# Layer 1 of a two-layer graph network: three gather tiles, two one-hot and message tiles, and new distances between its stages

## The chip, the core and the metric

The kernel runs on one core of a Trainium2 chip. A core has five engines, each with its own instruction queue worked through in order: TensorE (PE in the profile, with its weight loads as PEld), VectorE (DVE), ScalarE (ACT), GpSimd (POOL) and SyncE (SP, which here issues transfers only). Transfers are issued from the queues of SP, ACT and POOL. Engines wait for each other through semaphores. The metric is the device time of one execution in microseconds.

## The reference

There are 12,500 nodes with 48 features and 200,000 edges, sorted by their target node `dst`. Two layers follow each other, each ending in a residual sum and a layer norm over the features:

```
h   = relu(concat(x[dst], x[src], edge_attr_32) @ W1 + b1)
x   = layernorm(x + segment_sum(h @ W2 + b2, dst))            # layer 0
m   = relu(x[src] + edge_attr_48)
x   = layernorm(x + (1 + eps) * x + segment_sum(m, dst))      # layer 1
```

The change is in layer 1: for every edge a row of x (after layer 0) is gathered by `src`, the edge's 48 features are added, relu is taken, and the results are summed by `dst`.

## The kernel before

Edges are worked in 391 groups of 512: 128 partitions by 4 tiles (`TPC`). Nodes are worked in 14 segments of 896 (`SN`). Each layer is one call of `run(stages, ...)` (L485 on): a loop over iterations k, in which every stage (f, d) is called with group g = k - d, in the order of the list. The list thus writes out the order of the instructions of every engine by hand; the tile pools add the waits. A pool with n buffers of a name hands them out in turn, and whoever writes a buffer waits until the readers of its last use, n uses ago, are done.

Layer 0 gathers x rows (L222, by `fetch0`), multiplies and sums, and `finish0` (L395) ends a segment: the new rows x1 are stored to `x1_dram` by SP, and for all but the last segment also to `front_dram` by ACT.

Layer 1 has these stages:

- `fetch1(g)`: four indirect gathers on POOL (all have line L222), one for each tile of the group, into a tile `xs`. Groups 0 to 5 (`FRONT`) are gathered from `front_dram`, which lacks the last segment, so that they need not wait for it; these 24 gathers are issued near the end of layer 0. All others read `x1_dram`. `xs` has 12 buffers.
- `fill1(g)`: a one-hot matrix `hot` of the group's targets, on DVE (L530), ten buffers; and the group's edge features, which SP loads in chunks of five groups (`load_edges`, L314, tile `e48c`, three buffers). DVE reads `rel1` and `iota_1`, both in SBUF.
- `message1(g)`: m = xs + e48c on DVE (L539), for groups 0 to 5 a second add of `more` (L541), then the relu on ACT into `msg1` (L543), ten buffers.
- `sum1(g)`: four matmuls of `msg1` and `hot` on PE (L557; the profile counts two passes of each, eight rows) into a PSUM bank that twelve groups share (`GB`); a bank is opened and closed by a matmul of zeros (L554, L562).
- `drain1(g)`: for the last group of a bank, its columns are added or copied into `table` by DVE (L575) and ACT (L580). When a segment is complete, `finish1` follows: transposes on PE (L362), sums and layer norm on DVE with two steps on ACT (L420 to L390), and the store by SP (L425).

`lead1` is called at the end of an iteration. At k = -1, 1 and 3 it calls `last_segment` for two groups each: for the six front groups it looks up the rows of the last segment, which `front_dram` lacks, by one-hots `which_e` on DVE (L600), transposes on PE (L605), comparisons `o` on DVE (L621), matmuls (L613, L623) and a reduction `more` on DVE (L629). Eight iterations before a segment's last group it loads that segment's x1 rows (`load_seg`, L163).

The stages before stand in the order fetch1 (6 groups ahead), fill1 (2 ahead), sum1 (1 behind), drain1 (9 behind), message1 (0).

Of the kernel before, what the change touches and what calls it, by code (L numbers as in the profile page):

```python
# [27 lines left out]
F32 = mybir.dt.float32  # L28
# [6 lines left out]
P = 128  # L35
# [3 lines left out]
D = 48  # L39
# [6 lines left out]
TPC = 4  # L46
# [10 lines left out]
TAIL = 128  # L57
SROWS = HEAD + SN + TAIL
AHEAD = 6
NW = 8  # L60
EC = 5
R1 = 48
GB = 12
FRONT = 6
# [9 lines left out]
W1 = STEP + 2 * R1  # L74
# [19 lines left out]
def seg_of(g):  # L94
    return min(share(g) // SN, NSEG - 1)
# [10 lines left out]
@with_exitstack  # L106
def gnn_kernel(
    ctx: ExitStack,
    tc: tile.TileContext,
    x: bass.AP,  # L110
    src: bass.AP,
    dst: bass.AP,
    e32: bass.AP,
    e48: bass.AP,
    w1: bass.AP,
    b1: bass.AP,
    w2: bass.AP,
    b2: bass.AP,
    eps: bass.AP,
    out: bass.AP,  # L120
):
    nc = tc.nc
    flag_pool = ctx.enter_context(tc.tile_pool(name="flag", bufs=1))
    dram = ctx.enter_context(tc.tile_pool(name="dram", bufs=1, space=bass.MemoryType.DRAM))
    flag = flag_pool.tile([1, 1], I32, name="flag")
    with ExitStack() as fast:
        windowed(fast, tc, dram, flag, x, src, dst, e32, e48, w1, b1, w2, b2, eps, out)
    misfit = nc.values_load(
        flag, engines=[mybir.EngineType.PE, mybir.EngineType.DVE, mybir.EngineType.Activation,
                       mybir.EngineType.Pool, mybir.EngineType.SP],  # L130
        min_val=0, max_val=4 * P,
    )
    with tc.If(misfit > 0), ExitStack() as slow:
        general(slow, tc, dram, x, src, dst, e32, e48, w1, b1, w2, b2, eps, out)


def windowed(ctx, tc, dram, flag, x, src, dst, e32, e48, w1, b1, w2, b2, eps, out):
    nc = tc.nc
    const = ctx.enter_context(tc.tile_pool(name="const", bufs=1))
    cats = ctx.enter_context(tc.tile_pool(name="cats", bufs=AHEAD + 8))  # L140
    echunk = ctx.enter_context(tc.tile_pool(name="echunk", bufs=3))
    xs_pool = ctx.enter_context(tc.tile_pool(name="xs_pool", bufs=AHEAD + FRONT))
    late = ctx.enter_context(tc.tile_pool(name="late", bufs=10))
    work = ctx.enter_context(tc.tile_pool(name="work", bufs=3))
    aggs = ctx.enter_context(tc.tile_pool(name="aggs", bufs=3))
    node = ctx.enter_context(tc.tile_pool(name="node", bufs=2))
# [22 lines left out]
    nc.scalar.dma_start(w1a, w1[0:D, :])  # L169
    wcats = [const.tile([Q, HID], F32, name=f"wcat{k}") for k in range(NW)]  # L170
    for t in wcats:
# [41 lines left out]
    x1_dram = dram.tile([NPAD, D], F32, name="x1_dram")  # L213
# [7 lines left out]
    def gather(t, table, g, j):  # L221
        nc.gpsimd.indirect_dma_start(  # L222
            out=t, out_offset=None, in_=table,
            in_offset=bass.IndirectOffsetOnAxis(
                ap=src_i[:, g * TPC + j : g * TPC + j + 1], axis=0
            ),
        )
# [81 lines left out]
    def load_edges(name, table, width, g):  # L309
        c = g // EC  # L310
        if g % EC == 0:
            n = min(EC, NCHUNK - g)
            chunk[name] = echunk.tile([P, EC, TPC * width], F32, name=name)
            nc.sync.dma_start(  # L314
                chunk[name][:, :n, :],
                table[g * CHUNK : (g + n) * CHUNK, :].rearrange(
                    "(c p t) d -> p c (t d)", p=P, t=TPC
                ),
            )
        return chunk[name][:, g % EC, :].rearrange("p (t d) -> p t d", t=TPC)  # L320
# [10 lines left out]
    def start_of(engine, g):  # L331
        if (engine, g // 4) not in starts_of:
            kind = {nc.sync: mybir.EngineType.SP, nc.vector: mybir.EngineType.DVE}[engine]
            _, starts_of[engine, g // 4] = nc.values_load_multi_w_load_instructions(
                off[0:1, g // 4 * 4 : g // 4 * 4 + 4], engines=[kind], min_val=0,
                max_val=SROWS - W,
                skip_runtime_bounds_check_because="off is held to its range where it is made",
            )
        return starts_of[engine, g // 4][g % 4]
# [52 lines left out]
    def rows_of(table, s):  # L392
        return table[s * SN : (s + 1) * SN, :].rearrange("(t p) d -> p t d", p=Q)
# [42 lines left out]
    cat, h, pt, ph, pm, pa, hot = {}, {}, {}, {}, {}, {}, {}  # L436

    def fetch0(g):
        cat[g] = cats.tile([P, TPC, Q], F32, name="cat")
        for j in range(TPC):  # L440
            gather(cat[g][:, j, W : W + D], x, g, j)

    def fill0(g):
# [3 lines left out]
        nc.sync.dma_start(  # L447
            wcats[g % NW][0:W, :], a_dram[seg_of(g)][bass.ds(start_of(nc.sync, g), W), :]
        )
# [10 lines left out]
    def hidden0(g):  # L460
        ph[g] = psum.tile([HID, TPC, P], F32, name="ph", bufs=2)
        nc.tensor.matmul(ph[g], wcats[g % NW], h[g], start=True, stop=True)  # L462

# [21 lines left out]
    def run(stages, adds, finish, lead):  # L485


        last = max(d for _, d in stages)
        first = min(d for _, d in stages)
        for k in range(first, NCHUNK + last):  # L490
            for f, d in stages:
                g = k - d
                if 0 <= g < NCHUNK:
                    f(g)
                    if f is adds:
                        for s in finishes.get(g, []):
                            finish(s)
            lead(k)

    def lead0(k):  # L500
        for s in range(1, NSEG):
            if k == first_group(s - 1) + 4:
                load_seg(x, s)
            if k == first_group(s - 1) + 8:
                project(s)
        if k == 14:
            check_windows()
            nc.scalar.dma_start(rows_of(front_dram, NSEG - 1), none)
        if k == NCHUNK - AHEAD:
            for g in range(FRONT):  # L510
                fetch1(g, front_dram)

    def fetch1(g, table):
        cat[g] = xs_pool.tile([P, TPC, D], F32, name="xs")
        for j in range(TPC):
            gather(cat[g][:, j, :], table, g, j)

    for g in range(AHEAD):
        fetch0(g)
    project(0)  # L520
    run(
        [(lambda g: g >= AHEAD and fetch0(g), -AHEAD), (fill0, -2), (add0, 7), (sum0, 6),
         (bias0, 5), (message0, 4), (relu0, 3), (hidden0, 2), (turned0, 1), (turn0, 0)],
        add0, finish0, lead0,
    )


    def fill1(g):
        o = late.tile([P, TPC, W1], F32, name="hot")
        nc.vector.tensor_tensor(  # L530
            o, iota_1[:, None, :].to_broadcast([P, TPC, W1]),
            rel1[:, g, :, None].to_broadcast([P, TPC, W1]), op=ALU.is_equal,
        )
        hot[g] = o
        h[g] = load_edges("e48c", e48, D, g)

    def message1(g):
        m = work.tile([P, TPC, D], F32, name="m")
        nc.vector.tensor_tensor(m, cat.pop(g), h[g], op=ALU.add)  # L539
        if g in more:  # L540
            nc.vector.tensor_tensor(m, m, more.pop(g), op=ALU.add)  # L541
        msg = late.tile([P, TPC, D], F32, name="msg1")
        nc.scalar.activation(msg, m, AF.Relu)  # L543
        h[g] = msg

# [92 lines left out]
    def lead1(k):  # L638
# [4 lines left out]
                load_seg(x1_dram, s)  # L643

    run(
        [(lambda g: g >= FRONT and fetch1(g, x1_dram), -AHEAD), (fill1, -2), (sum1, 1), (drain1, 9), (message1, 0)],
        None, None, lead1,
    )

# [210 lines left out]
```

## Time and profile before

| | before |
|---|---|
| median of 3 runs | 3965.46 us (3963.3 to 3965.85) |
| profiled execution | 3967.04 us, its span 3965.3 us |
| POOL busy in the span | 2989.5 us (75%), 3138 instructions |
| PE busy | 2559.0 us (65%) |
| DVE busy | 1093.3 us (28%) |
| ACT busy | 560.3 us (14%) |
| granted PE clock, whole span | 0.645 of full |

The span runs from the first to the last instruction of the program. Layer 0 takes its first half; the gathers of layer 1 run from 1967.2 us to 3947.4 us. A row of a group gives its line, engine, operation and tiles, then how often it ran, busy microseconds, the mean of one in nanoseconds, and after the second bar how long the engine stood idle just before these instructions and what ended it. A row of the timeline gives the start, the duration, the engine, the line and the tiles, and in brackets the idle time before it and what ended it. A row of the waits names the engine and line that waited, what it waited for, the sum in microseconds, how often, and the longest. "issue" is time in which an engine waited for nothing that the profile shows.

### The profile page before, as it was taken

To read this page: it belongs to the slowest core of one execution; us is meant where nothing else is said; L and a number is where in the kernel's file an instruction comes from. 1 tells how busy PE (TensorE), PEld (TensorE's weight loads), DVE (VectorE), ACT (ScalarE), POOL (GpSimd) and SP (SyncE) were. 2 spreads that over 40 slices of the span, in tenths; PEclk is the share of its full clock that TensorE was granted. 3 is DMA by queue.
4 is the path that set the end of the run, shared out by engine and by line. 5 is a ranking of instruction groups with operands and counts; after the bars stand their busy time and mean duration, and the time that the engine had idled before them with its cause. 6 is when DMAs were issued, how large, how long until landed. Compare 5 with 4: busy or idle time off the path is not lost. (4 is left out here: it accounts for less than half of the span.)

```text
span 3965.3 us, 40239 instructions
## 1 busy us (share of the span) xinstructions
PE 2559.0 (65%) x12586; PEld 1748.8 (44%) x12586; DVE 1093.3 (28%) x2766; ACT 560.3 (14%) x1329; POOL 2989.5 (75%) x3138
## 2 busy tenths in 40 slices
PE   6888888888888888888874444444444444444444
PEld 4565555555555555555553333232233233333232
DVE  4233233323323332332252221222122222222122
ACT  1122112212212221221110000000000000000000
POOL 7777777777777777777777777777777777777776
PEclk8777787777778777877765555555555555555555
DMA  3122222212212221221121211111111121122121
GB/s 77 36 54 48 48 42 48 50 37 52 50 42 49 48 49 37 52 47 36 35 58 35 48 43 35 43 43 43 40 43 43 30 53 43 30 48 44 34 48 28
DMA packets 309612, 175.26 MB, mean 44 GB/s; under 512 B 124288, under 2 KB 309136, under 8 KB 309392
## 3 DMA queue, kind: packets, MB, share of 16 engines
q0 software_dynamic: 100096, 77.07, 11.2%
q1 hardware_dynamic: 179632, 84.47, 7.8%
q10 hardware_dynamic: 29664, 11.10, 1.1%
q8 instruction: 100, 1.64, 0.2%
q14 instruction: 120, 0.98, 0.1%
HBM read 157.37 MB, written 15.03 MB: 43 GB/s over the span
## 5 line engine op out<-in xcount | busy, mean ns | idle before, releaser
L222 POOL DMA_INDIRECT cat<-in_x_dram,src_i x1564 | 1483.2, 948 | 480.6 <-issue 336.8
L222 POOL DMA_INDIRECT xs<-x_dram,src_i x1540 | 1481.0, 962 | 469.3 <-issue 360.2
L557 PE MATMUL pt<-hot,msg 128*48 128x128 f32 x3128 | 743.7, 419 | 1059.7 <-ACT msg L543 1059.5
L557 PEld LDWEIGHTS pt<-hot,msg 128*48 128x48 f32 x3128 | 561.9, 194 | 1273.5 <-ACT msg L543 1249.7
L462 PE MATMUL ph<-cat_t,wcat 128*128 128x512 f32 x782 | 573.3, 824 | 0.9 <-DVE cat_t L458 0.9
L454 PE MATMUL pt<-ident,cat 128*128 128x128 f32 x1564 | 399.4, 348 | 266.8 <-DMA cat<-in_x_dram,src_i 261.7
L454 PEld LDWEIGHTS pt<-ident,cat 128*128 128x128 f32 x1564 | 263.9, 174 | 668.8 <-DMA cat<-in_x_dram,src_i 411.2
L539 DVE TENSOR_TENSOR m<-xs,e48c 128x192 f32<-128x192 f32 x391 | 146.2, 374 | 1433.3 <-DMA xs<-x_dram,src_i 1433.3
L471 PE MATMUL pm<-w_sb,h 128*128 128x48 f32 x3128 | 531.4, 323 | 1.8 <-ACT h L466 1.8
L458 DVE COPY cat_t<-pt 128x512 f32<-128x512 f32 x391 | 269.8, 690 | 883.1 <-PE pt L454 883.1
L471 PEld LDWEIGHTS pm<-w_sb,h 128*128 128x128 f32 x3128 | 478.0, 234 | 27.8 <-ACT h L466 2.1
L466 ACT ACTIVATE h<-ph,b_sb 128x512 f32<-128x512 f32 x391 | 268.4, 686 | 1340.1 <-PE ph L462 1306.6
L543 ACT ACTIVATE msg<-m 128x192 f32<-128x192 f32 x391 | 141.9, 363 | 1714.9 <-DVE m L539 1661.8
L530 DVE TENSOR_TENSOR hot<-iota,rel 128x512 f32<-128x512 f32 x391 | 266.5, 682 | 0.0
L354 PE MATMUL pa<-cat,msg 128*48 128x48 f32 x3128 | 260.6, 237 | 2.1 <-DVE agg L349 2.0
L354 PEld LDWEIGHTS pa<-cat,msg 128*48 128x48 f32 x3128 | 207.4, 147 | 77.1 <-issue 46.8
L475 DVE TENSOR_TENSOR msg<-pm,b_sb 128x192 f32<-128x192 f32 x391 | 139.2, 356 | 275.0 <-PE pm L471 274.8
L462 PEld LDWEIGHTS ph<-cat_t,wcat 128*128 128x128 f32 x782 | 153.4, 244 | 1.2 <-DVE cat_t L458 1.2
L323 DVE TENSOR_TENSOR cat<-iota_w,rel 128x192 f32<-128x192 f32 x391 | 136.2, 350 | 0.1
L445 ACT ACTIVATE cat<-e32c 128x128 f32<-128x128 f32 x391 | 117.0, 300 | 43.6 <-DMA e32c<-in_e_dram 14.2
L349 DVE TENSOR_TENSOR agg<-agg,pa 48x48 f32 x391 | 74.3, 190 | 17.0 <-PE pa L354 10.3
L293 PE MATMUL px<-w1a,xt 48*128 48x128 f32 x196 | 47.2, 407 | 20.2 <-ACT xt L290 20.2
(90 smaller groups left out, 607.0 us busy)
## 6 DMA issues: line engine op xcount, KB each, us to landing
e48c<-in_e_dram SPq DMA_DIRECT2D x78, 480.0 KB
cat<-in_x_dram,src_i POOLq DMA_INDIRECT x1564
e32c<-in_e_dram SPq DMA_DIRECT2D x78, 320.0 KB
xs<-x_dram,src_i POOLq DMA_INDIRECT x1540
wcat<-a SPq DMA_DIRECT2D x391, 24.0 KB
a<-a ACTq DMA_DIRECT2D x14, 256.0 KB
a<-a ACTq DMA_DIRECT2D x14, 192.0 KB
x_seg<-in_x_dram SPq DMA_DIRECT2D x14, 168.0 KB
```

Of the source, the lines that this page charges most:

```text
L222: nc.gpsimd.indirect_dma_start(out=t, out_offset=None, in_=table, in_offset=bass.IndirectOffsetOnAxis(ap=src_i[:, g * TPC + j : g * TPC + ...
L354: nc.tensor.matmul(pa, msg[:, j, :], hot[:, j, :], start=j == 0, stop=j == TPC - 1)
L454: nc.tensor.transpose(pt[g][:, j, :], cat[g][:, j, :], ident[:P, :P])
L458: nc.vector.tensor_copy(h[g], pt.pop(g))
L462: nc.tensor.matmul(ph[g], wcats[g % NW], h[g], start=True, stop=True)
L466: nc.scalar.activation(h[g], ph.pop(g), AF.Relu, bias=b1_sb)
L471: nc.tensor.matmul(pm[g][:, j, :], h[g][:, j, :], w2_sb, start=True, stop=True)
L475: nc.vector.tensor_tensor(h[g], pm.pop(g), b2_sb[:, None, :].to_broadcast([P, TPC, D]), op=ALU.add)
L530: nc.vector.tensor_tensor(o, iota_1[:, None, :].to_broadcast([P, TPC, W1]), rel1[:, g, :, None].to_broadcast([P, TPC, W1]), op=ALU.is_equal,)
L539: nc.vector.tensor_tensor(m, cat.pop(g), h[g], op=ALU.add)
L543: nc.scalar.activation(msg, m, AF.Relu)
L557: nc.tensor.matmul(bank[k][:, i * STEP : i * STEP + W1], msg[:, j, :], o[:, j, :], start=False, stop=False, skip_group_check=True,)
```

## The change

It touches layer 1 alone. Groups 0 to 5 get six gather tiles of their own name (`xs_front`); the others share three tiles `xs`, and their gathers stand two groups ahead in the order. `hot` and `msg1` come from a pool with two buffers each instead of ten. The edge load is a stage of its own, five groups ahead. The one-hot stands one group ahead instead of two, the sum in the message's own iteration and behind it, the drain three groups behind instead of nine, and behind message and sum instead of ahead of the message.

```diff
+AHEAD1 = 2
...
-    xs_pool = ctx.enter_context(tc.tile_pool(name="xs_pool", bufs=AHEAD + FRONT))
-    late = ctx.enter_context(tc.tile_pool(name="late", bufs=10))
+    xs_pool = ctx.enter_context(tc.tile_pool(name="xs_pool", bufs=AHEAD1 + 1))
+    pair = ctx.enter_context(tc.tile_pool(name="pair", bufs=2))
...
     def fetch1(g, table):
-        cat[g] = xs_pool.tile([P, TPC, D], F32, name="xs")
+        if g < FRONT:
+            cat[g] = xs_pool.tile([P, TPC, D], F32, name="xs_front", bufs=FRONT)
+        else:
+            cat[g] = xs_pool.tile([P, TPC, D], F32, name="xs")
...
+    def load1(g):
+        h[g] = load_edges("e48c", e48, D, g)
+
     def fill1(g):
-        o = late.tile([P, TPC, W1], F32, name="hot")
+        o = pair.tile([P, TPC, W1], F32, name="hot")
...
         hot[g] = o
-        h[g] = load_edges("e48c", e48, D, g)
...
-        msg = late.tile([P, TPC, D], F32, name="msg1")
+        msg = pair.tile([P, TPC, D], F32, name="msg1")
...
     run(
-        [(lambda g: g >= FRONT and fetch1(g, x1_dram), -AHEAD), (fill1, -2), (sum1, 1), (drain1, 9), (message1, 0)],
+        [(load1, -5), (lambda g: g >= FRONT and fetch1(g, x1_dram), -AHEAD1), (fill1, -1),
+         (message1, 0), (sum1, 0), (drain1, 3)],
         None, None, lead1,
     )
```

## The prediction

> **What bounds the kernel now.** I read the page first, then the waits, then the timeline, at the hand-over between the layers and in layer 1. From the page:
>
> ```profile
> span 3965.3 us, 40239 instructions
> L222 POOL DMA_INDIRECT xs<-x_dram,src_i x1540 | 1481.0, 962 | 469.3 <-issue 360.2
> L530 DVE TENSOR_TENSOR hot<-iota,rel 128x512 f32<-128x512 f32 x391 | 266.5, 682 | 0.0
> L539 DVE TENSOR_TENSOR m<-xs,e48c 128x192 f32<-128x192 f32 x391 | 146.2, 374 | 1433.3 <-DMA xs<-x_dram,src_i 1433.3
> ```
>
> The gathers of layer 1 take 1481.0 us and the 0.3 us of issue before each another 469.3: 1950 us, nearly the whole of the layer. DVE sits 1433.3 us waiting for gathered rows. So POOL's queue is the bound, and a microsecond in which POOL cannot issue is lost, as nothing after it has slack. The list of waits asks whether POOL ever waits for a buffer:
>
> ```profile
> DVE m L539 <- DMA xs<-x_dram,src_i: 1433.3, 362, 6.0
> POOL xs L222 <- DVE m L539: 3.0, 10, 0.3
> ```
>
> It does not: ten entries of 0.3 us, which is its issue time. With twelve xs tiles, the gathers of group g need m of group g-12. Now the hand-over, in order of time:
>
> ```profile
> 2007.51 2.23 DVE L600 TENSOR_SCALAR which_e<-iota,part,block 128x128 bf16<-128x128 f32 x8
> 2008.65 1.43 PE L605 MATMUL pa<-ident,which_e 128*128 128x128 bf16 x8
> 2012.49 0.94 POOL L222 DMA_INDIRECT xs<-x_dram,src_i  x1 [0.30 <-issue]
> 2023.92 0.35 DVE L539 TENSOR_TENSOR m<-xs,e48c 128x192 f32<-128x192 f32 x1
> 2024.58 0.68 DVE L530 TENSOR_TENSOR hot<-iota,rel 128x512 f32<-128x512 f32 x1
> 2024.70 0.36 ACT L543 ACTIVATE msg<-m 128x192 f32<-128x192 f32 x1 [16.71 <-DVE m L541]
> 2025.12 1.94 PE L557 MATMUL pt<-hot,msg 128*48 128x128 f32 x8 [0.33 <-ACT msg L543]
> 2025.85 2.13 DVE L600 TENSOR_SCALAR which_e<-iota,part,block 128x128 bf16<-128x128 f32 x8
> 2040.43 1.07 PE L557 MATMUL pt<-hot,msg 128*48 128x128 f32 x8
> 2044.07 0.35 DVE L539 TENSOR_TENSOR m<-xs,e48c 128x192 f32<-128x192 f32 x1
> 2045.27 1.44 POOL L222 DMA_INDIRECT xs<-x_dram,src_i  x1 [0.30 <-issue]
> ```
>
> Gathers from x1_dram start at 1997.41, four to a group, 1.25 us apart; counting them, the row at 2012.49 is the first of group 9. Counting the m rows from 2005.59 (group 0), 2023.92 is m of group 2 and 2044.07 m of group 6. The rows with which_e open the three look-ups of the last segment, some 16 us each, which hold DVE and PE until 2041. Here POOL ran far ahead of m: group 9 was issued 31 us before m of group 6. Last, a steady group and the end of a segment:
>
> ```profile
> 2060.41 0.94 POOL L222 DMA_INDIRECT xs<-x_dram,src_i  x1 [0.30 <-issue]
> 2066.69 0.36 DVE L539 TENSOR_TENSOR m<-xs,e48c 128x192 f32<-128x192 f32 x1 [4.04 <-DMA xs<-x_dram,src_i]
> 2196.20 0.51 DVE L420 TENSOR_TENSOR total<-px,x_seg 128x336 f32<-128x336 f32 x1 [2.57 <-PE px L362]
> 2200.24 0.51 DVE L390 TENSOR_TENSOR o<-ln_yc,ln_rstd 128x336 f32<-128x336 f32 x1
> 2201.15 1.29 POOL L222 DMA_INDIRECT xs<-x_dram,src_i  x1 [0.30 <-DVE m L539]
> ```
>
> 2060.41 is the first gather of group 18 and 2066.69 its m: 6.28 us from one to the other. A group takes four gathers, 4 x 1.25 = 5.0 us.
>
> **The change, part by part.** Layer 0 and the 24 front gathers keep their order and their tiles; 0.
>
> *Three xs tiles, at the hand-over.* Groups 0 to 5 have tiles of their own, groups 6, 7 and 8 find three free ones, and group 9 must wait for m of group 6. That wait is new. Without anything else m(6) ends at 2044.07 + 0.35 = 2044.42. With 0.30 of issue POOL starts group 9 at 2044.72 and not at 2012.49: 32.2 us, a floor, since the three look-ups are not shortened.
>
> *Two hot tiles.* The one-hot of group g now waits until PE has summed group g-2, and it stands on DVE ahead of m(g-1). So behind m(2), DVE waits for ACT and PE before the next one-hot and m(3). From the rows: m(2) 2023.92, ACT 2024.70 (0.78 later, the second add between), PE 2025.12 (0.42), sum 1.94, and 0.05 to the next start (an estimate from PE-to-DVE gaps of 0.03 to 0.06 in the timeline): 3.19 us, where before the next one-hot started 0.66 after m. That is 2.53 us more, or 1.66 where the sum takes 1.07, as at 2040.43. Before m(6) it happens four times: between m(0) and m(1), m(2) and m(3), m(4) and m(5), m(5) and m(6). In the other places the sum lies ahead of a look-up and is long done. I take the first two at 1.94 and the last two at 1.07, as the rows at these times have them: 2 x 2.53 + 2 x 1.66 = 8.4.
>
> *Sum at distance 0.* PE now sums the second group of a pair ahead of the next look-up's transposes. Before, these began 1.14 us after which_e (2007.51 to 2008.65). Now the sum ends 0.78 + 0.42 + 1.94 = 3.14 after m and which_e starts 0.66 after m, so they begin 2.48 after it: 1.3 later, for the second and the third look-up: 2.6. Bounds 0 and 2.6.
>
> *One-hot at -1 instead of -2.* One one-hot fewer stands ahead of the first look-up: minus 0.6 (their pitch there).
>
> So m(6) ends at 2044.42 + 8.4 + 2.6 - 0.6 = 2054.8, POOL starts group 9 at 2055.1, and the new wait is **42.6 us**. With all four sums slow it is 44.3; with all fast and no late transposes 38.3.
>
> *After it.* m(7) follows m(6) by a one-hot that waits for a sum, some 3.5 us, and m(8) as much later; the gathers of groups 10 and 11, 5.0 us apart, find their tiles free. So one stall, not a series. What was late before is regained in part: from 2012.49 to 2055.23 the gathers of groups 9 to 16 took 42.7 us for 32 x 1.25 = 40.0, five of them 1.44 us long, because DVE ran one-hots and adds end to end. DVE is paced by PE now; I leave 0.7 for chance collisions: minus 2.0 (0 to minus 2.8).
>
> *Steady groups.* POOL needs m(g-3) when it starts group g: 3 x 5.0 = 15.0 us after group g-3 began, and m ends 6.28 + 0.36 = 6.6 after that. 8.4 us of margin. DVE's new loop is m to ACT 0.45, to PE 0.42, sum 1.94, 0.05, one-hot 0.6: 3.5 us in a group of 5.0, hidden; if that cover went, every group would pay the excess. For msg1's two tiles ACT waits for a sum that is two groups old: 0.
>
> *Where the one-hot falls.* A gather that starts while a two-input DVE instruction runs is held until about 0.13 us before its end: a one-hot at 2200.94, 0.68 long, held the gather of 2201.15 to 1.29 us instead of 0.94. Before, it ran 0.3 us behind m; now 2.85 us behind it (0.45 + 0.42 + 1.94 + 0.05). m starts close to the start of a gather, so 2.85 - 2 x 1.25 = 0.35 into a later one, and it is done at 1.03, before the next start at 1.25: no hold. Added up over the timeline of before, the gathers that a one-hot held lost 8 us in all of layer 1, mostly behind late m's; sums late by a bank change will collide now and then. I take minus 2, bounds minus 8 and plus 15 (374 groups by 0.04 us, if all sums took 1.07 and the one-hot ended at 1.98 + 0.68 = 2.66, where the next gather starts at 2.50).
> The Trainium skill, SBUF — State Buffer, section Who interferes with whom, says that a DVE instruction with two SBUF inputs contends with a GpSimd instruction that reads SBUF and that whoever comes first keeps the ports for its whole instruction. The trace agrees for a gather that comes second; but one-hots run inside a 0.94 us gather, and m is lengthened to 0.43 us at most. By the rule a one-hot 0.35 into a gather would start at its end, 0.94, and hold the next until 1.63, not 1.25: 0.38 x 374 = 142 us slower, and the sum would be 4146; by the rows it is nothing.
>
> *Segment ends.* Thirteen times a finish blocks DVE. It now follows m(k) and its sum: sum done at 2.81, transposes 1.0, then total to o (2196.20 to 2200.75) 4.6, so DVE is free 8.4 us after m(k) started; the one-hot 0.6, and m(k+1) starts at 9.0 instead of 5.0. 4.0 late against 8.4 of margin, and 1.5 made up per group: 0. If the cover went, 13 times the excess.
>
> *Edge loads five ahead, drains three behind.* SP issues 79 loads earlier in its order, ahead of x_seg loads and out stores that they stood behind; no m waits for e48c in the list of waits, the load still waits for m of eleven groups before, and 11 groups are 55 us: 0. A drain three groups behind its sum comes over 10 us after it: 0. The tail after the last gather keeps its chain: 0.
>
> Sum: 42.6 - 2.0 - 2 = +38.6. The profiled execution took 3967.04 (span 3965.3), 1.6 over the median of the runs, 3965.46. I put the difference on the median: **4004**. Its own range: stall 38.3 to 44.3, give or take 2 for PE's clock in the look-ups, regained 0 to 2.8, one-hots minus 8 to plus 15: 3991 to 4027.
>
> **Rivals.**
> - *The one-hot meets gather starts.* PE's clock or the phase of m shifts it. For: 2201.15 shows the hold; the sum takes 1.07 at times. Against: granted clock 0.51 over 2055 to 3945, where nearly all sums take 1.94. A one-hot that fell anywhere would be in the way 0.51/1.25 of the time by 0.26 us on average, 0.106 x 374 = 40 us: 4044.
> - *Segment ends stall POOL.* If m(k+1) is over 8.4 us late, 13 times the excess; twice the 4.0 that I count and another 2 for a slow landing (DVE's longest wait for rows is 6.0, the usual one 4.2) gives 1.6 x 13 = 21 us: 4025.
> - *Not slower.* The place is the POOL row of layer 1: 962 ns mean against 944 in an undisturbed gather, 18 ns x 1540 = 28 us. If pacing took all of it, the stall would have to be under 28 to break even; its floor is 32.2. It would be a wash only at 3965.5 + 32.2 - 28 = 3970 at best. That group 9 does not wait for m(6) at all, which would mean no change, has only the order of buffers against it, and that is plain.
>
> **How the numbers follow.** Main case 0.83, one-hot collisions 0.08, segment ends 0.05, not slower 0.04 (0.02 for each side). Faster 0.02, same (within 0.2%, 8 us, about what a measurement of this kernel can tell) 0.02, slower 0.96. The range is the main case's own, a microsecond wider at the top: 3991 to 4028 leaves out the first rival's 40 us.
>
> **What would show it.** POOL idle once, about 43 us from 2012.5, ended by DVE m; x_dram gathers back to back afterwards, with no further waits for m above 1 us; DVE's one-hots waiting for PE sums at L557's successor; the mean of a gather between 944 and 975 ns; the last gather about 39 us later than 3946.5. The forecast is wrong if POOL waits for m at segment ends, or if that mean passes 975.

## The result, and the profile after

The changed kernel takes 4005.68 us, median of four runs (4003.38 to 4010.75), against 3965.65 us before (3963.3 to 3966.2): a ratio of 1.0103, with a 95% interval of 1.009 to 1.0116. The forecast was 4004 us, with a range of 3991 to 4028. The profiled execution took 4003.38 us, the fastest of the four; its span is 4001.4 us. The profile before is of an execution of 3967.04 us, so the two profiles differ by 36.1 us in their spans where the medians differ by 40.0.

Lines in the profile after have moved: L223 is the gather (before L222), L537 the one-hot (L530), L545 m (L539), L549 the relu (L543), L563 the sum (L557), L606 which_e (L600), L611 its transposes (L605), L421 to L391 the end of a segment (L420 to L390).

From the page of the changed kernel:

```profile
span 4001.4 us, 40613 instructions
L223 POOL DMA_INDIRECT xs<-x_dram,src_i x1540 | 1480.2, 961 | 508.1 <-issue 299.3
L537 DVE TENSOR_TENSOR hot<-iota,rel 128x512 f32<-128x512 f32 x391 | 270.7, 692 | 942.7 <-PE pt L563 942.7
```

A gather is as long as before, 961 ns against 962. What POOL idled ahead of its gathers grew from 469.3 to 508.1 us. The one-hot, which never waited, now waits 942.7 us for PE, and DVE has that time: its wait for gathered rows falls from 1433.3 to 489.5 us. The list of waits of the changed kernel says where POOL's 39 us are, as engine, line, what it waited for, and then the sum, the number and the longest:

```profile
DVE hot L537 <- PE pt L563: 942.7, 374, 3.6
DVE m L545 <- DMA xs<-x_dram,src_i: 489.5, 342, 4.9
POOL xs L223 <- DVE m L545: 39.5, 2, 39.2
```

Two waits for m, one of 39.2 us, the other an issue time of 0.3: a single stall. The timeline of the changed kernel at the hand-over, in order of time, shows its two ends:

```profile
2005.69 2.13 DVE L606 TENSOR_SCALAR which_e<-iota,part,block 128x128 bf16<-128x128 f32 x8
2008.10 1.03 PE L611 MATMUL pa<-ident,which_e 128*128 128x128 bf16 x8
2009.98 0.94 POOL L223 DMA_INDIRECT xs<-x_dram,src_i  x1 [0.30 <-issue]
2041.73 0.35 DVE L545 TENSOR_TENSOR m<-xs_front,e48c 128x192 f32<-128x192 f32 x1
2043.01 1.94 PE L563 MATMUL pt<-hot,msg 128*48 128x128 f32 x8 [2.31 <-ACT msg L549]
2044.99 0.69 DVE L537 TENSOR_TENSOR hot<-iota,rel 128x512 f32<-128x512 f32 x1 [2.51 <-PE pt L563]
2045.60 0.35 DVE L545 TENSOR_TENSOR m<-xs_front,e48c 128x192 f32<-128x192 f32 x1
2048.85 0.69 DVE L537 TENSOR_TENSOR hot<-iota,rel 128x512 f32<-128x512 f32 x1 [2.51 <-PE pt L563]
2049.46 0.35 DVE L545 TENSOR_TENSOR m<-xs,e48c 128x192 f32<-128x192 f32 x1
2050.08 0.94 POOL L223 DMA_INDIRECT xs<-x_dram,src_i  x1 [39.16 <-DVE m L545]
```

2009.98 is the last gather of group 8. 2041.73, 2045.60 and 2049.46 are m of groups 4, 5 and 6; from one to the next the message, its sum and the next one-hot follow each other, 3.87 us a step where the kernel before took 1.26. Then m(6) releases group 9.

The 36.1 us between the two profiled spans can be laid out by the starts of gathers. The gathers of group 6 began 1.7 us earlier (1995.75 against 1997.41). From there to the first of group 9 it took 54.33 us against 15.08: 39.2 more. From there to the first of group 20, 56.1 against 57.9: 1.8 less. From there to the end of the last gather, 1877.6 against 1877.0: 0.5 more, in 371 groups. The tail took 0.2 less.

The end of a segment in the timeline of the changed kernel:

```profile
2203.04 0.42 DVE L545 TENSOR_TENSOR m<-xs,e48c 128x192 f32<-128x192 f32 x1 [1.37 <-DMA xs<-x_dram,src_i]
2206.88 0.51 DVE L421 TENSOR_TENSOR total<-px,x_seg 128x336 f32<-128x336 f32 x1 [3.19 <-PE px L363]
2211.36 0.69 DVE L537 TENSOR_TENSOR hot<-iota,rel 128x512 f32<-128x512 f32 x1
2211.96 0.35 DVE L545 TENSOR_TENSOR m<-xs,e48c 128x192 f32<-128x192 f32 x1
2213.16 0.94 POOL L223 DMA_INDIRECT xs<-x_dram,src_i  x1 [0.31 <-issue]
```

m starts 8.9 us after the one ahead of it (8.9 to 9.1 at the thirteen segment ends; 8.2 to 8.5 in the kernel before; 5.0 within a segment), and POOL goes on without a wait.

### The profile page after: what moved, and what is told of

It is laid out like the page before. It is cut to its first block, busy times and chain, and to the rows that moved or that the text cites. A ratio compares the mean times of both kernels' runs of the same rounds, so it can differ in the third digit from the quotient of the medians.

```text
span 4001.4 us, 40613 instructions
## 1 busy us (share of the span) xinstructions
PE 2564.6 (64%) x12586; PEld 1746.7 (44%) x12586; DVE 1125.6 (28%) x2766; ACT 557.4 (14%) x1329; POOL 2987.1 (75%) x3138
## 4 chain that ended last, share of the span: by engine, by line
DMA 37%; POOL 23%; PE 19%; issue 12%; DVE 5%; ACT 3%; ACTq 0%; POOLq 0%; DVEq 0%
DMA cat<-in_x_dram,src_i 19%; DMA xs<-x_dram,src_i 18%; POOL xs L223 11%; POOL cat L223 11%; PE pt L563 7%; PE pm L472 3%; PE ph L463 3%; DVE hot L537 2%; PE pa L355 2%; PE pt L455 2%; DVE m L545 1%; ACT msg L549 1%; PE px L294 1%; POOL xs_front L223 1%; ACT cat L446 0%
## 5 line engine op out<-in xcount | busy, mean ns | idle before, releaser
L223 POOL DMA_INDIRECT xs<-x_dram,src_i x1540 | 1480.2, 961 | 508.1 <-issue 299.3
L223 POOL DMA_INDIRECT cat<-in_x_dram,src_i x1564 | 1481.8, 947 | 480.6 <-issue 342.3
L563 PE MATMUL pt<-hot,msg 128*48 128x128 f32 x3128 | 758.5, 424 | 1086.4 <-ACT msg L549 1086.3
L563 PEld LDWEIGHTS pt<-hot,msg 128*48 128x48 f32 x3128 | 567.6, 195 | 1310.0 <-ACT msg L549 1284.7
L537 DVE TENSOR_TENSOR hot<-iota,rel 128x512 f32<-128x512 f32 x391 | 270.7, 692 | 942.7 <-PE pt L563 942.7
L549 ACT ACTIVATE msg<-m 128x192 f32<-128x192 f32 x391 | 141.8, 363 | 1763.7 <-DVE m L545 1636.2
L545 DVE TENSOR_TENSOR m<-xs,e48c 128x192 f32<-128x192 f32 x385 | 144.1, 374 | 489.8 <-DMA xs<-x_dram,src_i 489.5
L568 PE MATMUL pt<-zeros 1*48 1x480 f32 x66 | 60.4, 1016 | 0.0
```

The lines of the kernel that those rows point to most:

```text
L223: nc.gpsimd.indirect_dma_start(out=t, out_offset=None, in_=table, in_offset=bass.IndirectOffsetOnAxis(ap=src_i[:, g * TPC + j : g * TPC + ...
L537: nc.vector.tensor_tensor(o, iota_1[:, None, :].to_broadcast([P, TPC, W1]), rel1[:, g, :, None].to_broadcast([P, TPC, W1]), op=ALU.is_equal,)
L563: nc.tensor.matmul(bank[k][:, i * STEP : i * STEP + W1], msg[:, j, :], o[:, j, :], start=False, stop=False, skip_group_check=True,)
```

## The experiments

Three questions were open: whether the stall is all of it and follows the number of gather tiles, how much of it each part of the change makes, and whether the place of the one-hot between the gathers is as harmless as it was priced. Unless another kernel is named, an edit is to the changed kernel. The first four runs fell on a chip on which the kernel before takes 4785.65 us; what they showed stands at the end of this section. Three of the four edits were run again on another chip. All other times are beside 3965 to 3967 us for the kernel before.

**Twelve gather tiles instead of three.**

```diff
-    xs_pool = ctx.enter_context(tc.tile_pool(name="xs_pool", bufs=AHEAD1 + 1))
+    xs_pool = ctx.enter_context(tc.tile_pool(name="xs_pool", bufs=12))
```

> [...] Theory as before: 3967 to 3970 us, no wait of POOL for m. Rival (the two hot tiles or the order cost along the layer): 3990 or more.

Measured: 3969.75 us (3966.26 to 3972.8), 1.0012 of the kernel before (1.0002 to 1.0021). POOL's waits for m are gone: the list of waits of this run has four entries for m, none longer than the 0.3 us that lie between any two gathers (the first line, too, is made of such intervals):

```profile
POOL xs L223 <- DVE hot L537: 60.0, 197, 0.3
...
POOL xs L223 <- DVE m L545: 1.2, 4, 0.3
```

So 36 of the 40 us come back with nothing but gather tiles, though hot, msg1 and the order stay as changed. The 4 us that remain are just over what can be told from nothing, and this profile, of the fastest of ten executions (3966.26), does not show them. In it DVE works off its backlog at 3.5 us a group until group 35, and one-hots held gathers for 13.4 us in all, against 8.2 before, m's for 12.5 against 16.5 (each gather's time above 944 ns, added up over the timeline from 2080 us on).

**Seven gather tiles.** The same edit with bufs=7.

> [...] Theory: the wait moves from group 9 to group 13 and lasts 39.2 - 20.1 = 19 us; 3983 to 3990 us.

Measured: 3988.52 us (3987.56 to 3994.01), 1.0061 (1.0044 to 1.0078). The line of POOL's waits for m in this run:

```profile
POOL xs L223 <- DVE m L545: 18.6, 3, 18.0
```

The wait is 18.0 us against 39.2 with three tiles, 5.3 us a tile, where the theory says 5.03. The time falls by 17. The wait and the time both follow the number of tiles: the stall is POOL running out of tiles while DVE is held by the look-ups.

**The gather tiles alone, in the kernel before.**

```diff
+AHEAD1 = 2
...
-    xs_pool = ctx.enter_context(tc.tile_pool(name="xs_pool", bufs=AHEAD + FRONT))
+    xs_pool = ctx.enter_context(tc.tile_pool(name="xs_pool", bufs=AHEAD1 + 1))
...
-        cat[g] = xs_pool.tile([P, TPC, D], F32, name="xs")
+        if g < FRONT:
+            cat[g] = xs_pool.tile([P, TPC, D], F32, name="xs_front", bufs=FRONT)
+        else:
+            cat[g] = xs_pool.tile([P, TPC, D], F32, name="xs")
...
-        [(lambda g: g >= FRONT and fetch1(g, x1_dram), -AHEAD), (fill1, -2), (sum1, 1), (drain1, 9), (message1, 0)],
+        [(lambda g: g >= FRONT and fetch1(g, x1_dram), -AHEAD1), (fill1, -2), (sum1, 1), (drain1, 9), (message1, 0)],
```

> [...] Theory: a wait of 32 us, less what comes back of the burst: 3995 (3990 to 3999). The run with ten hot and msg1 tiles should be its twin but for the order of sums (3992.5 there). Rival (two hot tiles alone make the wait): under 3975.

Measured: 3996.64 us (3994.73 to 3999.14), 1.0079 (1.0062 to 1.0096). The list of waits has one stall, of 31.1 us:

```profile
POOL xs L223 <- DVE m L543: 33.8, 10, 31.1
```

This is the floor of the prediction, 32.2: the look-ups alone, from the first which_e (1988.13) to m(6) (2042.63) 54.5 us, as before (54.75). By themselves these tiles make 31 of the 40 us.

**Ten hot and msg1 tiles instead of two.**

```diff
-    pair = ctx.enter_context(tc.tile_pool(name="pair", bufs=2))
+    pair = ctx.enter_context(tc.tile_pool(name="pair", bufs=10))
```

> The changed kernel with ten hot and ten msg1 tiles in place of two, three xs tiles left. Theory: the one-hots ahead of m(6) no longer wait for sums, which took 9.8 us (four times the step from one m to the next, 3.35 + 3.75 + 3.87 + 3.86 less 4 x 1.26), so the wait of group 9 falls from 39.2 to about 29.5 and the time to 3996 (3992 to 4000). Rival (two tiles cost nothing, the late transposes and the look-ups make it all): 4003 or more.

Measured: 3992.53 us (3988.36 to 3998.35), 1.0061 (1.0044 to 1.0078). The profiled execution, the slowest of the four at 3998.35, has its first look-up and m(6) at these places of the timeline, and one wait of POOL for m:

```profile
1993.26 2.23 DVE L606 TENSOR_SCALAR which_e<-iota,part,block 128x128 bf16<-128x128 f32 x8
2046.00 0.35 DVE L545 TENSOR_TENSOR m<-xs,e48c 128x192 f32<-128x192 f32 x1
```

```profile
POOL xs L223 <- DVE m L545: 33.5, 1, 33.5
```

From the first look-up to m(6) it takes 52.7 us; in the changed kernel, 1985.71 to 2049.46, 63.75. So with the two small pools the chain is 11.0 us longer, of which 9.8 are the four one-hots that wait for sums; the other 1.2 lie in the look-ups. The stall was nevertheless 33.5 us and not 29.5: here the first look-up began 5.0 us before the first gather of group 6 (1998.23), in the profile of the changed kernel 10.0, and before 8.1. How far layer 0's end on DVE and PE lies behind POOL differs, though no edit touches layer 0: the first look-up began 3.7 to 11.2 us before the first gather of group 6 in the profiles beside 3965 to 3967 us. With twelve tiles POOL does not wait, with three this difference goes into the wait. Whether it also widens the spread of the times is not shown: the kernels with three tiles spread by 4.4 to 10 us, but those with twelve by 5.1 and 6.5, and only one execution of each was profiled.

**The order alone.** Twelve xs tiles and four hot and msg1 tiles; the stages stay as changed.

```diff
-    xs_pool = ctx.enter_context(tc.tile_pool(name="xs_pool", bufs=AHEAD1 + 1))
-    pair = ctx.enter_context(tc.tile_pool(name="pair", bufs=2))
+    xs_pool = ctx.enter_context(tc.tile_pool(name="xs_pool", bufs=12))
+    pair = ctx.enter_context(tc.tile_pool(name="pair", bufs=4))
```

> The changed order alone: twelve xs tiles and four hot and msg1 tiles, with edge loads five ahead, one-hots one ahead, sums at distance 0, drains three behind. Theory: none of these lies on POOL's path; 3965.7 +- 2. Rival (the new order costs by itself, by segment ends or edge loads): 3972 or more.

Measured: 3965.03 us (3962.05 to 3967.18), 0.9996 (0.9986 to 1.0005). Edge loads, one-hots, sums and drains in their new places cost nothing that can be told from noise. The run with twelve gather tiles differs from this one in the two small pools alone, and each beside the kernel before on its chip they are some 6 us apart (+4.4 and -1.7). So the rest of the loss seems to go with these pools; the two intervals overlap slightly, which leaves it unproven.

**One-hots 0.54 us and 1.08 us later.** One reduction into the hot tile, overwritten by the one-hot, is put ahead of it; in the second kernel two.

```diff
         o = pair.tile([P, TPC, W1], F32, name="hot")
+        nc.vector.tensor_reduce(o[:, 0, :NB], none, AX.X, ALU.add)
```

> The changed kernel with one reduction of 128x336 to 128x7 written into the hot tile ahead of each one-hot, so that the one-hot starts about 0.54 us later. Theory (phase): it starts 2.87 + 0.54 = 3.41 us after m, 0.91 us into a gather, ends 0.35 us after the start of the next, and holds it 0.22 us (its end less 0.13): 374 x 0.22 = 82 us, so 4075 to 4100, with the mean of a gather near 1010 ns. Rival (DVE only has to have time, 4.0 us of a 5.0 us group): 4006.

> The same with two such reductions, so that the one-hot starts about 1.08 us later. Theory (phase): 3.95 us after m is 0.2 us after the start of a later gather, so the one-hot runs inside it, ends 0.88 us into it and holds nothing; DVE's loop is 4.6 us of 5.0. Close to the changed kernel, 4003 to 4025, although there is twice as much additional DVE work as in the run with one. Rival (more DVE work, more loss): well above the run with one reduction.

Measured: with one reduction 4046.01 us (4043.46 to 4048.56), 40.3 more than the changed kernel; with two 4027.23 (4023.54 to 4029.98), 21.6 more. The second does more on DVE and costs less, which the rival excludes. Part of both is the stall, 45.4 and 56.3 us against 39.2:

```profile
POOL xs L223 <- DVE m L546: 45.4, 1, 45.4
```

```profile
POOL xs L223 <- DVE m L547: 60.9, 16, 56.3
```

From the first which_e to m(6) it takes 70.8 and 74.1 us instead of 63.75, and with two reductions the first look-up happened to begin only 3.7 us before the first gather of group 6 and not 10.0, which makes 6.3 of that stall. The rest is in the gathers; the groups of the two pages, one reduction first, then two:

```profile
L223 POOL DMA_INDIRECT xs<-x_dram,src_i x1540 | 1514.3, 983 | 514.4 <-issue 309.6
```

```profile
L223 POOL DMA_INDIRECT xs<-x_dram,src_i x1540 | 1488.1, 966 | 525.2 <-issue 285.5
```

983 ns a gather against 961 is 34 us over 1540 gathers, 966 is 8. The direction is as expected, the size with one reduction is under half of the 82 us. The timeline of that run shows why:

```profile
2604.11 0.69 DVE L538 TENSOR_TENSOR hot<-iota,rel 128x512 f32<-128x512 f32 x1
2604.42 1.20 POOL L223 DMA_INDIRECT xs<-x_dram,src_i  x1 [0.30 <-DVE hot L537]
2605.63 0.36 DVE L546 TENSOR_TENSOR m<-xs,e48c 128x192 f32<-128x192 f32 x1 [0.83 <-DMA xs<-x_dram,src_i]
2609.04 0.69 DVE L538 TENSOR_TENSOR hot<-iota,rel 128x512 f32<-128x512 f32 x1
2609.68 0.94 POOL L223 DMA_INDIRECT xs<-x_dram,src_i  x1 [0.30 <-issue]
```

The first one-hot holds the gather of 2604.42 to 1.20 us. All gathers after it start later by that much, but m of the next group waits for rows gathered before and starts on time, at 2605.63; so its one-hot falls 0.27 us earlier between the gathers and clears the next start (2609.04 + 0.68 = 2609.72, less 0.13, is before 2609.68). About every second group is held: from 2080 us on 186 of some 370, 0.27 us each, 50 us in all against 11 in the changed kernel. The alternation is not strict: about a third of the held groups follow another held one. The step that the expectation left out, as these rows show it, is that a hold shifts the phase that caused it.

**A version that beats both: m 0.2 us later, in the kernel before.** Nothing of the output depends on the added instruction.

```diff
         m = work.tile([P, TPC, D], F32, name="m")
+        last = node.tile([P, 1], F32, name="most")
+        nc.vector.tensor_scalar(last, cat[g][:, TPC - 1, 0:1], 1.0, None, op0=ALU.mult)
```

> The kernel before with one more DVE instruction per group in layer 1: one column of the group's last gathered tile, times 1, into a spare 128x1 tile, ahead of m. Nothing of the output depends on it. It takes the wait for the last gather, so m starts some 0.15 to 0.25 us later. Theory (phase): m then starts inside a gather and not just before its start, and the 16.6 us that m held gathers in the profile of before go, while one-hots that follow m still end before the next start: 3945 to 3955. Rival (the holds only move to the next gather or to the one-hot): 3960 to 3970. If the one-hot is pushed over the next start: above 3970.

Measured: 3948.06 us (3946.05 to 3948.85), 0.9957 of the kernel before (0.9942 to 0.9971). The gathers' group on its page:

```profile
L222 POOL DMA_INDIRECT xs<-x_dram,src_i x1540 | 1461.0, 949 | 469.1 <-issue 357.3
```

And one group of layer 1 in its timeline:

```profile
2599.88 0.15 DVE L540 TENSOR_SCALAR most<-xs 128x1 f32<-128x1 f32 x1 [3.83 <-DMA xs<-x_dram,src_i]
2599.91 0.94 POOL L222 DMA_INDIRECT xs<-x_dram,src_i  x1 [0.30 <-issue]
2600.08 0.36 DVE L541 TENSOR_TENSOR m<-xs,e48c 128x192 f32<-128x192 f32 x1
2600.36 0.68 DVE L530 TENSOR_TENSOR hot<-iota,rel 128x512 f32<-128x512 f32 x1
```

m now starts 0.17 us after the start of a gather, where it used to fall on it or just before. A gather takes 949 ns instead of 962: 13 ns x 1540 = 20 us, and 17 are measured. Added up over the timeline from 2080 us on, m's held gathers for 0.1 us instead of 16.5, one-hots for 2.7 instead of 8.2. 391 more instructions on an engine that has time make the kernel faster.

**The first four runs, on another chip.** The changed kernel again, and the first tries with twelve tiles, seven tiles and the gather tiles alone.

> The changed kernel once more, on the chip of the next three. Theory (one stall): POOL waits once, between groups 8 and 9, for m of group 6, 39 to 43 us, and nowhere else over 1 us; 4001 to 4011 us. Rival (the tight coupling costs all along the layer): the same time, but spread, with POOL waits for m at segment ends or a slower pitch of the gathers. If the spread of the changed kernel's times (7 us against 3 us of the kernel before) comes from the hand-over, the length of this wait differs from the first profile's 39.2 by about what the span differs.

> The changed kernel with twelve xs tiles in place of three, all else as changed. Theory: group 9 finds a free tile, the wait of 39.2 us goes, and of the 1.8 us that came back behind it most is lost again, since DVE works off its backlog beside the gathers: 3967 to 3970 us. Rival (cost all along the layer, by two hot tiles, the new order or segment ends): 3990 us or more, as all of these are still in.

> The changed kernel with seven xs tiles. Theory: group 13 is the first to wait for m of group 6; four groups more, 4 x 5.03 = 20.1 us, are issued before the wait, so it lasts 39.2 - 20.1 = 19 us, and the time is about 3986 (3983 to 3990). If tiles acted otherwise than through this one wait, the time would not fall by 5 us a tile.

> The kernel before with one part of the change alone: own tiles for the six front groups and three xs tiles (gathers two groups ahead in the order); one-hots, messages, sums, drains and edge loads as before. Theory: POOL waits only for the three look-ups, the floor of the prediction, 32.2 us; of the burst's 2.8 us most comes back: 3965.7 + 32.2 - 2.5 = 3995 (3990 to 3999). Rival (two hot tiles alone make the wait): under 3975.

Measured: the changed kernel 4807.68 us, 1.0048 (1.0032 to 1.0065); twelve tiles 4823.73, 1.0074 (1.0052 to 1.0096); seven 4809.35, 1.0053 (1.0033 to 1.0072); the gather tiles alone 4788.2, 0.9999 (0.9978 to 1.0019). None of the expected numbers holds. Three lines of the waits of the changed kernel there:

```profile
DVE hot L537 <- remote: 1011.2, 119, 13.8
POOL xs L223 <- DVE m L545: 330.7, 66, 61.4
DVE m L545 <- DMA xs<-x_dram,src_i: 2.6, 3, 1.0
```

A gather lasts 971 ns, hardly more than elsewhere, but POOL waits for m 66 times all along the layer, 330.7 us, and DVE's one-hots wait 1011 us, in stretches of up to 13.8, for something that the profile does not name ("remote"). Slow gathered rows are not what holds it up: DVE waits 2.6 us for them, and the page of that profile gives the gathers' queue 9.0% of 16 DMA engines over 4803.3 us, no more time than the 11.0% over 4001.4 us elsewhere. Of the 802 us between the two profiles of the changed kernel, 485 had passed by the first gather of group 6 (2480.56 against 1995.75), most of it in layer 0, which the change leaves alone. POOL is not the bound there, and what the bound is stays open. Two readings hold all the same: a change of tiles that costs 0.8% where POOL is the bound costs nothing there, and the changed kernel with twelve gather tiles is no better there than with three (16 us worse), so that its loss on that chip is not the gather tiles. Whether it is the two small pools or the order was not tested there.

## Why the prediction was right

The single stall was forecast at 42.6 us and is 39.2. The mechanism, its place and its end (m of group 6 releasing group 9) are as stated; its terms were off in both directions. The four one-hots that wait for sums were put at 8.4 us and took 9.8 (steps from m to m of 3.35, 3.75, 3.87 and 3.86 less 1.26 each). The first two sums took 1.51 and 1.82 us and not 1.94, the last two 1.94 and not 1.07: the row at 2040.43 ran where the granted clock was 1.00 (2040 to 2042), and from 2042 to 2050 it is now 0.50. PE also idles longer ahead of these two sums (2.31 and 1.92 us, against 1.23 before the sum of 2042.74 in the kernel before); that this is the reason is not shown. The late transposes were put at 2.6 and took 1.9 (their ends 3.44 and 3.52 us after which_e, against 2.57 and 2.47). The look-ups themselves, given 0 with 2 us either way for PE's clock, took 2.7 less, which is outside that allowance: the zero matmuls that open the third (four rows of the profile) took 1.89 and not 3.25 us. Together, from the first which_e to m(6), 63.75 against 54.75, where 11.0 more were forecast; and this which_e began 2.0 us earlier against the gathers, for which 0.6 were forecast: 32.2 + 9.0 - 2.0 = 39.2.

Regained behind the stall: 2.0 forecast, 1.8 measured.

The place of the one-hot: minus 2 forecast, and 0.5 us more were measured over the rest of the layer. From 2080 us on, one-hots held gathers for 10.6 us instead of 8.2, and m's for 14.7 instead of 16.5, so the sign of this small term was wrong. The one-hot starts 2.87 us after m (forecast 2.85), half of them 0.40 us or more into a gather, and the median gather takes 944 ns. The 142 us that the prediction estimated from the whole-instruction lock of the Trainium skill's SBUF — State Buffer, section Who interferes with whom, did not come: one-hots that started 0.10 to 0.15 us into a gather ran 0.69 us beside it. That a one-hot in the wrong place has a price is shown by the run with one reduction.

Segment ends, 0: m(k+1) starts 8.9 to 9.1 us after m(k), 9.0 forecast, and no wait of POOL follows. Edge loads, order of sums and drains, 0: the run with the order alone is at 0.9996.

None of the rivals took place where POOL is the bound: one-hots hold gathers for 2 us more and not 40, POOL waits at no segment end, and a gather is as long as before, so no pacing made up for the stall. That twelve gather tiles bring back 36 us and the gather tiles alone cost 31 fits this.

That the forecast lies within 1.7 us of the median is in part luck. The stall was put 3.4 us too high, the one-hot's place 2.5 too low, a start of group 6 that was 1.7 earlier was not foreseen, and the medians differ by 3.9 more than the profiles. The 1.7 us are also less than the spread of the changed kernel.

## What to carry to other kernels

When a queue is the bound, the buffers that it fills set how long any other engine may be busy without stopping it: add up the longest stretch in which the consumer is held (here 47 us from the first gather of group 6 to m(6) in the kernel before and 54 in the changed one, in the look-ups) and divide by the queue's pace, and do this for the hand-over and not for the steady state alone, where three tiles were enough. Chains inside that stretch, such as a one-hot that waits for a sum two groups back, count in full although they hide everywhere else. And look at which instruction of another engine is running at the moment when the bounding one starts: moving m by 0.2 us was worth 17 us here, where the rearranged order alone was worth nothing that could be measured.

## What the runs showed of the hardware that was not expected

- The prediction's rule on holds (2201.15: 1.29 us instead of 0.94) has a limit. In the profile before, 140 gathers that started while m or a one-hot ran were held, all by one that had been running for 0.04 us or more, to about 0.13 us before its end. Another 101 started 0.044 us or less after it and were not held; m then took up to 0.43 us instead of 0.36. Holds partly undo themselves: each shifts the gathers against m, so that with one-hots placed to hold a gather in every group about half did.
- On one chip the kernel before takes 4786 instead of 3966 us. The changed kernel, profiled there, has gathers of nearly the same length and stalls of DVE of up to 13.8 us ahead of one-hots that the profile puts down to no engine. The cause is open.
